# Placing the large loads behind an edge exchange on the sync queue, in a fused coupled-map-lattice, NCA and gate kernel

## The chip, the cores and the metric

The kernel runs on one core of a Trainium2 chip. The metric is the device time of one execution in microseconds. Times inside an execution come from its hardware profile. Engines are named as there: PE is TensorE, DVE is VectorE, ACT is ScalarE, POOL is GpSimd, SP is SyncE, which does nothing here but issue DMAs.

## The reference

Input is x, 32 images of 8 channels and 256 x 256 pixels, float32. Layer 0 normalises x by groups and computes three things of it: a coupled map lattice, an NCA, and a gate that mixes the two. Layer 1 is a quantised 3 x 3 convolution.

```python
x0 = group_norm(x)
grid = drive = x0
for _ in range(15):                                   # the lattice
    mapped = 3.9 * grid * (1.0 - grid)
    local = conv3x3(mapped, K_local, per channel)
    grid = 0.85 * (0.7 * mapped + 0.3 * local) + 0.15 * drive
cml = clip(grid, 0.0001, 0.9999)
nca = sigmoid(conv1x1(relu(conv3x3(x0, Wp, bp)), Wu, bu))
gin = concatenate([x0, cml, nca])                     # 24 channels
g = sigmoid(conv1x1(relu(conv3x3(gin, Wg1, bg1)), Wg2, bg2))
x = x + g * cml + (1.0 - g) * nca
x = x + dequantised(conv3x3(quantised(group_norm(x)), quantised(weight))) + bias
```

## The kernel before

The images are worked on in 8 groups of 4. The first large stage (`one`) runs for each group g three kinds of work beside one another: the lattice of group g, the NCA of the same group, and the gate of group g-1; the normalisation of group g+1 (`prep`) goes in between. Python generators emit the instructions of these, and `together` and `both` weave them by the weights that each `yield` gives. The order on PE is the order of emission (`manual_schedule` for PE); on the other engines and on the sync queue a scheduler places the instructions ahead of the run, in an order near that of emission, and each queue is then worked off in order. The last group's gate runs alone after the last lattice, and a second stage (`two`) does layer 1.

**Lattice.** One unit is one channel of the four images of a group, in two streams s = 0 and s = 1 of two images each; a unit has 15 steps, and in each step `half` runs for s = 0 and then for s = 1. A half is 16 small matmul pairs into PSUM on PE (L502) with three tiny `mark` matmuls (L277), two DVE operations that add the drive (L513), and two that apply the map (L523). The state has two layouts. In a half of the kind a2b, which holds if step + s is even, it goes from `m_a` to `m_b`, and POOL masks the edge columns (L528). In the other kind it goes from `m_b` to `m_a`, and `exchange` copies the edge rows between tiles inside `m_a` by two DMAs on the sync queue (L477, L478). The stream's next half reads `m_a`, so PE waits for these DMAs if they are late. Between a half and the next one of the same stream lies one half of the other stream.

`background(4)` issues up to four queued small DMAs after each half: loads of the next unit's drive (`d_a`, `d_b`) and stores of the last unit's result (L465).

**NCA.** An image has 8 tiles of 32 rows. `rows` loads a tile into one of two buffers `im` by four DMAs of 384 KB (L569), one tile ahead: it is called for tile t+1 after the first matmul group of tile t. `hidden` runs the 3 x 3 convolution on PE (L588), ACT applies the relu into `h` (L596), and `drain` does the 1 x 1 convolution (L604).

**Gate.** Also 8 tiles an image. `inputs` loads `gin` and `gnc` by three DMAs of 384 KB (L665, two buffers), one tile ahead; `blend` loads `mix` by two (L675, one buffer). PE convolves `gin` and `gnc` (L767); `arrange` computes from `mix` on ACT (L688) and POOL (L690, L692) what DVE then combines with the gate (L725, L726). Steps of one tile that are off PE are put into `chores`, of which `together` runs one after each half.

All of these DMAs, and the stores of the normalisation, of the NCA and of the gate, are issued on the sync queue.

Of the kernel before, what the change touches and what calls it, by code (L numbers as in the profile page):

```python
# [31 lines left out]
F32 = mybir.dt.float32  # L32
# [8 lines left out]
P = 128  # L41
C = 8
# [11 lines left out]
ROW = 2 * C * W  # L54
PART = PROWS * C * W
# [5 lines left out]
NBUF = 3 * GB  # L61
# [48 lines left out]
def kernel(  # L110
# [15 lines left out]
    nc = tc.nc  # L126
# [3 lines left out]
    def dram_ap(t, offset, dims):  # L130
        return bass.AP(t.tensor, t.offset + offset, dims)
# [30 lines left out]
    xp_s = [dp.tile([PROWS, 2, C, W], F32, name=f"xp_s{i}") for i in range(NBUF)]  # L162
# [3 lines left out]
    with tc.tile_pool(name="prep", bufs=1) as pp, tc.tile_pool(name="prep2", bufs=2) as pp2:  # L166
# [23 lines left out]
        for t, at, n, w, rows in (  # L190
# [4 lines left out]
            k = 64  # L195
# [59 lines left out]
    with ExitStack() as one:  # L255
# [30 lines left out]
        m_a = [fixed([P, TU, NJ + 2], f"m_a{i}") for i in range(2)]  # L286
# [108 lines left out]
        def lattice(g):  # L395
# [67 lines left out]
            def background(n):  # L463
                for _ in range(min(n, len(later))):
                    nc.sync.dma_start(*later.pop(0))  # L465
                    n -= 1
                    issued[0] += 1
                if g == 0 and units.keys() - {0}:
                    for _ in range(min(n, len(borders))):
                        nc.sync.dma_start(*borders.pop(0))  # L470

            def exchange(t):

                t = t.rearrange("p (k t) j -> p k (t j)", k=2)
                n = (NT - 1) * (NJ + 2)
                above, below = slice(0, n), slice(NJ + 2, NJ + 2 + n)
                nc.sync.dma_start(t[0::16, :, below], t[14::16, :, above])  # L477
                nc.sync.dma_start(t[15::16, :, above], t[1::16, :, below])  # L478

            JOBS = ((0, 5), (5, 10), (10, 14), (14, 18))  # L480
            HALVES = ((slice(0, 10), 5), (slice(10, 18), 4))
# [1 line left out]
            def half(c, step, s, d, m_a, m_b):  # L483

                a2b = (step + s) % 2 == 0
                n = NJ + 1 if a2b else NJ
                k = 0 if a2b else 1
                two = [unit(), unit()]

                def blocks(j, diagonal, first):  # L490
                    t0, t1 = JOBS[j]
                    pt = two[j // 2][:, j % 2, : (t1 - t0) * n].rearrange("p (t j) -> p t j", j=n)
                    own = m_a[:, t0:t1, 1 : 2 + NJ] if a2b else m_b[:, t0:t1, 0:NJ]
                    beside = m_a[:, t0:t1, 0 : 1 + NJ] if a2b else m_b[:, t0:t1, 1 : 1 + NJ]
                    if diagonal:
                        parts = ((LOW, LOW, k, own), (HIGH, HIGH, k, own))
                    elif a2b:
                        parts = ((LOW, HIGH, k, own), (HIGH, LOW, 2, beside))
                    else:
                        parts = ((HIGH, LOW, k, own), (LOW, HIGH, 2, beside))  # L500
                    for src, dst, w, rhs in parts:
                        T.matmul(pt[dst], lw[src, c, w, dst], rhs[src], start=first, stop=not first)  # L502

                for n_, (o, dg, first) in enumerate(((1, 0, True), (3, 2, True), (0, 1, False), (2, 3, False))):
                    blocks(o, False, first)
                    blocks(dg, True, first)
                    if n_ < len(MARKS):
                        mark(n_)

                gts = []  # L510
                for pt, (ts, w) in zip(two, HALVES):
                    gt = gp.tile([P, 10 * (NJ + 1)], F32, name="gt", tag="gt")[:, : 2 * w * n]
                    V.scalar_tensor_tensor(  # L513
                        gt.rearrange("p (u c) -> p u c", u=2), pt[:, :, : w * n], FLOOR,
                        d[:, ts, :].rearrange("p (u t) j -> p u (t j)", u=2), ALU.max, ALU.add,
                    )
                    gts.append(gt.rearrange("p (t j) -> p t j", j=n))
                for gt, (ts, w) in zip(gts, HALVES):
                    if step == STEPS - 1:
                        V.tensor_scalar(d[:, ts, :], gt, 0.0001, 1.0 - 0.0001, ALU.max, ALU.min)  # L520
                        continue
                    to = m_b[:, ts, :] if a2b else m_a[:, ts, 1 : 1 + NJ]
                    V.scalar_tensor_tensor(to, gt, 1.0, gt, ALU.subtract, ALU.mult)  # L523
                if step == STEPS - 1:
                    return a2b
                if a2b:
                    edge = m_b[:, :, 0 : NJ + 1 : NJ]
                    G.tensor_tensor(edge, edge, junk.unsqueeze(1).to_broadcast([P, TU, 2]), ALU.mult)  # L528
                else:
                    exchange(m_a)  # L530
                return a2b

            if g == 0:
# [24 lines left out]
            stored[g] = issued[0] + len(later)  # L558
            if g == NG - 1:
                background(len(later))  # L560

        ORDER = ((0, 4, 1, 5), (2, 6, 3, 7))

        def rows(b, t):

            im = ims[(NT8 * b + t) % 2]
            for k in range(2):
                for q in range(2):
                    nc.sync.dma_start(  # L569
                        im.bitcast(F32)[64 * q : 64 * q + 48, k, :, 1 : 1 + W],  # L570
                        dram_ap(
                            xp_s[b % NBUF], (32 * t + 16 * k + 8 * q) * ROW, [[W, 48], [ROW, 8], [1, W]]
                        ),
                    )
            return im

        loaded = {}

        def nca(b):
# [43 lines left out]

            ahead = loaded.pop(b, None) or rows(b, 0)
            for t in range(NT8):
                im = ahead
                acc = ps_a.tile([P, 512], F32, name="acc", tag="acc")
                for i in range(4):
                    hs = {}
                    for n in (i, i + 4):  # L630
                        hs[n], hs[n + 8] = hidden([im[64 * q : 64 * q + 48, :, n, :] for q in range(2)])
                        if n == 0:
                            if t < NT8 - 1:
                                ahead = rows(b, t + 1)
                            elif all((b + 1, g) in ready for g in range(4)):
                                loaded[b + 1] = rows(b + 1, 0)
                        yield 1.4
                    if i == 2 and done:
                        nc.sync.dma_start(*done)
                        done = None  # L640
                    if pend:
                        done = drain() or done
                    pend = (acc, t, i, hs)
                    yield 0.9
# [14 lines left out]
        def inputs(b, t):  # L659

            src = gs_s[b % NBUF]
            gin = gip.tile([96, 8, W], F32, name="gin", tag="gin")
            gnc = gip.tile([48, 8, W], F32, name="gnc", tag="gnc")
            for j, to in enumerate((gin[:48], gin[48:], gnc)):
                nc.sync.dma_start(  # L665
                    to, dram_ap(src, j * PART + 32 * t * C * W, [[W, 48], [4 * C * W, 8], [1, W]])
                )
            return gin, gnc

        def blend(b, t):  # L670

            src = gs_s[b % NBUF]
            mix = gip.tile([P, 3, 2, W], F32, name="mix", tag="mix", bufs=1)
            for k in range(2):
                nc.sync.dma_start(  # L675
                    mix[:, :, k, :],
                    dram_ap(src, (32 * t + 16 * k + 1) * C * W, [[W, P], [PART, 3], [1, W]]),
                )
            return mix

        flat = lambda t: t.rearrange("p k w -> p (k w)")

        def arrange(sc, mix):

            d = wk.tile([P, 512], F32, name="d", tag="d", bufs=1)
            f = wk.tile([P, 512], F32, name="f", tag="f", bufs=1)
            halves = (slice(0, W), slice(W, 512))
            S.activation(f, flat(mix[:, 0]), AF.Identity, bias=sc[:, 0:1], scale=sc[:, 2:3])  # L688
            for k, cols in enumerate(halves):
                G.tensor_tensor(d[:, cols], mix[:, 1, k], mix[:, 2, k], ALU.subtract)  # L690
            for k, cols in enumerate(halves):
                G.tensor_tensor(f[:, cols], f[:, cols], mix[:, 2, k], ALU.add)  # L692
            return d, f
# [14 lines left out]
        def gate(b):  # L708
# [36 lines left out]
            sc, ahead = staged.pop(b)  # L745
            last = None
            for t in range(NT8 + 1):
                while chores:
                    chores.pop(0)()
                now = {}  # L750
# [2 lines left out]
                    now["gt"] = opened(two[:, 1, :], last["r1"])  # L753
                    now["was"] = last
                if t < NT8:
                    (gin, gnc), mix = ahead
                    if t < NT8 - 1:
                        now["ahead"] = [inputs(b, t + 1)]
                    elif (b + 1) % GB:
# [18 lines left out]
                    was["y"] = mixed(now["gt"], *was["df"])  # L778

                def arrange_(now):  # L780
                    now["df"] = arrange(sc, now["mix"])

                def blend_(now):
                    if now["t"] < NT8 - 1:
# [24 lines left out]
                ahead = now.get("ahead")  # L809
# [89 lines left out]
        for g in range(NG):  # L899
            fill, t = images(nca, g), T_NCA  # L900
            if g:
                fill, t = both(fill, t, after(g - 1, images(gate, g - 1)), T_GATE), t + T_GATE
            if g + 1 < NG:
                fill, t = both(fill, t, prep(g + 1), T_PREP), t + T_PREP
# [176 lines left out]
```

## Time and profile before

| | |
|---|---|
| median of 3 runs | 12252.35 us (12244.07 to 12260.76) |
| profiled execution | 12231.09 us, of it span 12229.3 us |
| PE busy | 10809.9 us, 88% of the span |
| DVE, ACT, POOL busy | 7826.2, 3791.0, 1577.2 us |
| mean granted PE clock | 0.948 |
| DMA queue q1 (the sync queue) | 1651.64 MB, 66.0% of 16 engines' span |

The span is the time from the first to the last instruction of the program; the profiled execution's own time is 1.8 us more. The first group's lattice lasts until about 1585 us, the last one's until about 11280 us. In a line of a group of instructions, the fields are line, engine, operation, out<-in, shapes, count, then busy time in us, mean ns of one, and the idle time of the engine before them with what ended most of it. In a line of a timeline the first two numbers are start and duration in us, and brackets hold the idle time before and its releaser. In a line of the waits: engine and instruction, what it waited for, then total us, times and longest us. In a line of windows: the stretch, its length, then busy us and count for PE, PEld, DVE, ACT and POOL, the granted PE clock, the DMA engines' busy share and GB/s.

### The profile page before, as it was taken

The numbers are of one execution on the slowest core, as the hardware profiler recorded it, in microseconds if no ns is written. First come the engines' busy times: TensorE is split into PE (matmuls) and PEld (weight loads), VectorE is DVE, ScalarE is ACT, GpSimd is POOL, SyncE is SP. The second block draws the span as 40 slices with busy tenths as digits, with TensorE's granted clock in tenths as the row PEclk, the third lists the DMA queues.
The fourth block names the chain that finished last, engine by engine and source line by source line (L and its number), as shares of the span: only waits on it lengthen the run. The fifth ranks groups of instructions, "written<-read, shape, count | busy, mean of one in ns | idle before, by whom it ended". The sixth has DMA issues, their size and how long they took to land. (4 is left out here: it accounts for less than half of the span.)

```text
span 12229.3 us, 289998 instructions
## 1 busy us (share of the span) xinstructions
PE 10809.9 (88%) x124192; PEld 6033.0 (49%) x124192; DVE 7826.2 (64%) x11376; ACT 3791.0 (31%) x4034; POOL 1577.2 (13%) x2242
## 2 busy tenths in 40 slices
PE   4888899999999999999999999999999999999854
PEld 2544555555555555555555555555555555554222
DVE  4655666666666666666666666666666666665377
ACT  2222233332333333333333333333333333332133
POOL 1000011111111111111111111111111111111200
PEclk7999999999999999999999999999999999999776
DMA  6545567766777667766776667777677666665988
GB/s 171 97 98 102 101 136 147 143 140 138 147 142 148 137 137 145 151 141 134 148 151 139 135 140 147 143 145 149 133 146 149 141 133 129 126 123 114 204 249 259
DMA packets 2473159, 1759.74 MB, mean 144 GB/s; under 512 B 1021280, under 2 KB 2442944, under 8 KB 2471744
## 3 DMA queue, kind: packets, MB, share of 16 engines
q1 hardware_dynamic: 2380096, 1651.64, 66.0%
q10 hardware_dynamic: 91776, 89.53, 2.3%
q8 instruction: 979, 16.04, 0.6%
q14 instruction: 308, 2.52, 0.1%
HBM read 1130.62 MB, written 473.89 MB: 131 GB/s over the span
## 5 line engine op out<-in xcount | busy, mean ns | idle before, releaser
L596 ACT ACTIVATE h<-pt,bp_sb 128x1024 f32<-128x1024 f32 x2048 | 2275.6, 1113 | 4947.7 <-PE pt L588 4944.3
L588 PE MATMUL pt<-im,wp_hi 48*128 48x512 f32 x12288 | 2631.8, 424 | 165.4 <-ACT h L596 116.6
L502 PE MATMUL pt<-m_a,lw 64*64 64x325 f32 (+1 forms) x30720 | 2299.3, 433 | 464.9 <-DMA m_a<-m_a 410.1
L513 DVE SCALAR_TENSOR_TENSOR gt<-pt,d_b 128x650 f32<-128x650 f32 (+1 forms) x1920 | 1463.5, 763 | 1945.0 <-PE pt L502 1931.7
L588 PE MATMUL pt<-im,wp_lo 48*128 48x512 f32 x12288 | 2442.5, 393 | 0.2 <-issue 0.2
L513 DVE SCALAR_TENSOR_TENSOR gt<-pt,d_a 128x640 f32<-128x640 f32 (+1 forms) x1920 | 1447.2, 754 | 1531.5 <-PE pt L502 1528.2
L502 PE MATMUL pt<-m_b,lw 64*64 64x320 f32 (+1 forms) x30720 | 2200.5, 417 | 118.1 <-DVE gt L513 82.1
L502 PEld LDWEIGHTS pt<-m_a,lw 64*64 64x64 f32 x30720 | 1316.6, 138 | 1193.2 <-issue 596.9
L588 PEld LDWEIGHTS pt<-im,wp_hi 48*128 48x128 f32 x12288 | 1163.6, 185 | 1275.4 <-issue 719.4
L502 PEld LDWEIGHTS pt<-m_b,lw 64*64 64x64 f32 x30720 | 1237.4, 134 | 858.4 <-issue 463.5
L523 DVE SCALAR_TENSOR_TENSOR m_a<-gt 128x640 f32<-128x640 f32 (+1 forms) x1792 | 1431.7, 799 | 58.6
L523 DVE SCALAR_TENSOR_TENSOR m_b<-gt 128x650 f32<-128x650 f32 (+1 forms) x1792 | 1384.6, 774 | 101.3 <-DVE gt L513 2.8
L528 POOL TENSOR_TENSOR m_b<-m_b,junk 128x36 f32<-128x36 f32 x896 | 243.8, 272 | 7994.9 <-DVE m_b L523 5672.1
L588 PEld LDWEIGHTS pt<-im,wp_lo 48*128 48x128 f32 x12288 | 1168.7, 186 | 201.7 <-issue 0.6
L604 PE MATMUL acc<-h,wu_z 128*32 128x512 f32 x8192 | 1107.7, 612 | 0.0
L767 PE MATMUL pt<-gin,gw 96*32 96x384 f32 (+2 forms) x10240 | 772.0, 450 | 201.3 <-ACT gate L719 178.0
L277 PE MATMUL mark<-qw 64*64 64x1 bf16 x5760 | 947.6, 165 | 0.0
L277 PEld LDWEIGHTS <-qw 64*64 64x64 bf16 x5760 | 632.4, 110 | 205.4 <-issue 9.8
L767 PE MATMUL pt<-gnc,gw 48*32 48x126 f32 (+2 forms) x10240 | 733.1, 429 | 0.0
L767 PEld LDWEIGHTS pt<-gin,gw 96*32 96x32 f32 x10240 | 313.8, 115 | 823.7 <-issue 425.2
L690 POOL TENSOR_TENSOR d<-mix 128x256 f32<-128x256 f32 x512 | 552.1, 1095 | 1240.8 <-DVE gate L725 840.1
L767 PEld LDWEIGHTS pt<-gnc,gw 48*32 48x32 f32 x10240 | 295.0, 108 | 420.8 <-issue 415.3
(110 smaller groups left out, 5939.0 us busy)
## 6 DMA issues: line engine op xcount, KB each, us to landing
im<-xp_s SPq DMA_DIRECT2D x1024, 384.0 KB
gin<-gs_s SPq DMA_DIRECT2D x512, 384.0 KB
mix<-gs_s SPq DMA_DIRECT2D x512, 384.0 KB
gnc<-gs_s SPq DMA_DIRECT2D x256, 384.0 KB
d_a<-gs_s SPq DMA_DIRECT2D x2048, 36.0 KB
yb<-y_s ACTq DMA_DIRECT2D x28, 2432.0 KB
xr<-in_x_dram SPq DMA_DIRECT2D x128, 512.0 KB
xp_s<-hi SPq DMA_DIRECT2D x256, 256.0 KB
```

The lines of the kernel that those rows point to most:

```text
L277: T.matmul(one_[dst], qw[src, 0, dst], qw[src, 0, 0:1], start=True, stop=True)
L502: T.matmul(pt[dst], lw[src, c, w, dst], rhs[src], start=first, stop=not first)
L513: V.scalar_tensor_tensor(gt.rearrange("p (u c) -> p u c", u=2), pt[:, :, : w * n], FLOOR, d[:, ts, :].rearrange("p (u t) j -> p u (t j)", ...
L523: V.scalar_tensor_tensor(to, gt, 1.0, gt, ALU.subtract, ALU.mult)
L528: G.tensor_tensor(edge, edge, junk.unsqueeze(1).to_broadcast([P, TU, 2]), ALU.mult)
L588: T.matmul(ph[:, i, :].rearrange("p (h w) -> p h w", w=W), w[64 * i : 64 * i + 48, dx, :], rhs[:, :, dx : dx + W], start=(dx == 0 and w is ...
L596: S.activation(h.rearrange("p i c -> p (i c)"), ph.rearrange("p i c -> p (i c)"), AF.Relu, bias=bp_sb)
L604: T.matmul(acc[32 * g : 32 * g + 32], wu_z[:, 24 - 8 * i : 56 - 8 * i], hs[4 * g + i], start=(i == 0), stop=(i == 3),)
L690: G.tensor_tensor(d[:, cols], mix[:, 1, k], mix[:, 2, k], ALU.subtract)
L767: T.matmul(three[32 * i : 32 * i + 32, :, to], gw[:rows_, j, dx, :], src[:, i::4, of], start=(j == 0 and n == 0), stop=(j == 1 and n == le ...
```

## The change

`rows`, `inputs` and `blend` no longer issue their loads. Each returns a list of jobs, a job being a size in KB and the arguments of the DMA, and `ask` puts these into a list `asked`. `exchange` returns its second DMA, and `feed` then takes jobs from the front of `asked` as long as a budget of 1200 KB is above zero, and issues them with a scheduling dependency (without a semaphore) on that DMA, so that they stand behind it on the sync queue. Where a tile's computation is emitted, `settle` issues those of its jobs that no exchange has taken yet. After the last lattice `ask` issues at once, as before. Neither the DMAs nor the buffers nor any computation change.

```diff
--- before.py
+++ after.py
@@ -469,13 +469,22 @@
                     for _ in range(min(n, len(borders))):
                         nc.sync.dma_start(*borders.pop(0))
 
+            def feed(behind):
+
+                room = 1200
+                while asked and room > 0:
+                    job = asked.pop(0)
+                    if job[1]:
+                        room -= job[0]
+                        tc.add_manual_dep(begun(job).ins, behind.ins.name, BEHIND, reason="behind the exchange")
+
             def exchange(t):
 
                 t = t.rearrange("p (k t) j -> p k (t j)", k=2)
                 n = (NT - 1) * (NJ + 2)
                 above, below = slice(0, n), slice(NJ + 2, NJ + 2 + n)
                 nc.sync.dma_start(t[0::16, :, below], t[14::16, :, above])
-                nc.sync.dma_start(t[15::16, :, above], t[1::16, :, below])
+                return nc.sync.dma_start(t[15::16, :, above], t[1::16, :, below])
 
             JOBS = ((0, 5), (5, 10), (10, 14), (14, 18))
             HALVES = ((slice(0, 10), 5), (slice(10, 18), 4))
@@ -527,7 +536,7 @@
                     edge = m_b[:, :, 0 : NJ + 1 : NJ]
                     G.tensor_tensor(edge, edge, junk.unsqueeze(1).to_broadcast([P, TU, 2]), ALU.mult)
                 else:
-                    exchange(m_a)
+                    feed(exchange(m_a))
                 return a2b
 
             if g == 0:
@@ -558,21 +567,50 @@
             stored[g] = issued[0] + len(later)
             if g == NG - 1:
                 background(len(later))
+                alone.append(True)
+                settle(asked)
 
         ORDER = ((0, 4, 1, 5), (2, 6, 3, 7))
 
+        asked, alone = [], []
+        BEHIND = mybir.DependencyInfo(mybir.DependencyClass.NoSync, mybir.DependencyReason.DATA)
+
+        def begun(job):
+            args, job[1] = job[1], None
+            return nc.sync.dma_start(*args)
+
+        def settle(jobs):
+            for job in jobs:
+                if job[1]:
+                    begun(job)
+
+        def ask(jobs):
+            if alone:
+                settle(jobs)
+            else:
+                asked.extend(jobs)
+            return jobs
+
         def rows(b, t):
 
             im = ims[(NT8 * b + t) % 2]
-            for k in range(2):
-                for q in range(2):
-                    nc.sync.dma_start(
-                        im.bitcast(F32)[64 * q : 64 * q + 48, k, :, 1 : 1 + W],
-                        dram_ap(
-                            xp_s[b % NBUF], (32 * t + 16 * k + 8 * q) * ROW, [[W, 48], [ROW, 8], [1, W]]
+            return im, ask(
+                [
+                    [
+                        384,
+                        (
+                            im.bitcast(F32)[64 * q : 64 * q + 48, k, :, 1 : 1 + W],
+                            dram_ap(
+                                xp_s[b % NBUF],
+                                (32 * t + 16 * k + 8 * q) * ROW,
+                                [[W, 48], [ROW, 8], [1, W]],
+                            ),
                         ),
-                    )
-            return im
+                    ]
+                    for k in range(2)
+                    for q in range(2)
+                ]
+            )
 
         loaded = {}
 
@@ -623,7 +661,8 @@
 
             ahead = loaded.pop(b, None) or rows(b, 0)
             for t in range(NT8):
-                im = ahead
+                im, jobs = ahead
+                settle(jobs)
                 acc = ps_a.tile([P, 512], F32, name="acc", tag="acc")
                 for i in range(4):
                     hs = {}
@@ -661,26 +700,38 @@
             src = gs_s[b % NBUF]
             gin = gip.tile([96, 8, W], F32, name="gin", tag="gin")
             gnc = gip.tile([48, 8, W], F32, name="gnc", tag="gnc")
-            for j, to in enumerate((gin[:48], gin[48:], gnc)):
-                nc.sync.dma_start(
-                    to, dram_ap(src, j * PART + 32 * t * C * W, [[W, 48], [4 * C * W, 8], [1, W]])
-                )
-            return gin, gnc
+            return gin, gnc, ask(
+                [
+                    [
+                        384,
+                        (to, dram_ap(src, j * PART + 32 * t * C * W, [[W, 48], [4 * C * W, 8], [1, W]])),
+                    ]
+                    for j, to in enumerate((gin[:48], gin[48:], gnc))
+                ]
+            )
 
         def blend(b, t):
 
             src = gs_s[b % NBUF]
             mix = gip.tile([P, 3, 2, W], F32, name="mix", tag="mix", bufs=1)
-            for k in range(2):
-                nc.sync.dma_start(
-                    mix[:, :, k, :],
-                    dram_ap(src, (32 * t + 16 * k + 1) * C * W, [[W, P], [PART, 3], [1, W]]),
-                )
-            return mix
+            return mix, ask(
+                [
+                    [
+                        384,
+                        (
+                            mix[:, :, k, :],
+                            dram_ap(src, (32 * t + 16 * k + 1) * C * W, [[W, P], [PART, 3], [1, W]]),
+                        ),
+                    ]
+                    for k in range(2)
+                ]
+            )
 
         flat = lambda t: t.rearrange("p k w -> p (k w)")
 
-        def arrange(sc, mix):
+        def arrange(sc, mix, jobs):
+
+            settle(jobs)
 
             d = wk.tile([P, 512], F32, name="d", tag="d", bufs=1)
             f = wk.tile([P, 512], F32, name="f", tag="f", bufs=1)
@@ -753,7 +804,8 @@
                     now["gt"] = opened(two[:, 1, :], last["r1"])
                     now["was"] = last
                 if t < NT8:
-                    (gin, gnc), mix = ahead
+                    (gin, gnc, jobs), mix = ahead
+                    settle(jobs)
                     if t < NT8 - 1:
                         now["ahead"] = [inputs(b, t + 1)]
                     elif (b + 1) % GB:
@@ -778,7 +830,7 @@
                     was["y"] = mixed(now["gt"], *was["df"])
 
                 def arrange_(now):
-                    now["df"] = arrange(sc, now["mix"])
+                    now["df"] = arrange(sc, *now["mix"])
 
                 def blend_(now):
                     if now["t"] < NT8 - 1:
```

## The prediction

> **What bounds the kernel now.** I read the page first, then the windows by stage, the waits, and the timeline around the long PE gaps.
>
> ```profile
> PE 10809.9 (88%) x124192; PEld 6033.0 (49%) x124192; DVE 7826.2 (64%) x11376; ACT 3791.0 (31%) x4034; POOL 1577.2 (13%) x2242
> L502 PE MATMUL pt<-m_a,lw 64*64 64x325 f32 (+1 forms) x30720 | 2299.3, 433 | 464.9 <-DMA m_a<-m_a 410.1
> q1 hardware_dynamic: 2380096, 1651.64, 66.0%
> ```
>
> ```profile
> 200.00:1585.00 1385.00, 1169.98 (x13004) 695.88 (x13002) 820.71 (x1197) 391.96 (x381) 79.33 (x148) 0.92 0.51 99
> 1585.00:11280.00 9695.00, 9022.83 (x106937) 5078.63 (x106937) 6328.65 (x9410) 3072.90 (x3205) 1336.05 (x1886) 0.98 0.70 140
> ```
>
> From 1585 to 11280 us PE is busy 93% of the time: in the lattice stage PE sets the pace, and whatever stops it is paid almost in full. The largest stop is the exchange: 410.1 us of PE waiting for m_a<-m_a. That is all that this change can win back directly. All large loads share q1 with the exchange.
>
> The waits of the sync queue's own instructions show the place where SP stands most, at the first DMA of an exchange, for the DVE result. It is idle there, not overloaded:
>
> ```profile
> SPq L477 <- DVE m_a L523: 3298.4, 732, 14.8
> ```
>
> How a load hurts is best seen where the kernel before already does what the change makes a rule: four im loads right behind an exchange. The sync queue's timeline, then PE's, then windows of the clock (the value after POOL):
>
> ```profile
> 5424.63 0.63 SPq L477 DMA_DIRECT2D m_a<-m_a  x1
> 5425.31 0.62 SPq L478 DMA_DIRECT2D m_a<-m_a  x1
> 5426.03 1.93 SPq L569 DMA_DIRECT2D im<-xp_s  x4
> 5428.40 0.62 SPq L477 DMA_DIRECT2D m_a<-m_a  x1
> ```
>
> ```profile
> 5431.88 0.39 PE L588 MATMUL pt<-im,wp_lo 48*128 48x512 f32 x2
> 5438.98 1.79 PE L502 MATMUL pt<-m_a,lw 64*64 64x325 f32 x11 [6.71 <-DMA m_a<-m_a]
> ```
>
> ```profile
> 5424.00:5432.00 8.00, 7.88 (x98) 4.88 (x93) 6.06 (x9) 2.57 (x3) 0.00 (x0) 1.00 0.71 113
> 5432.00:5439.00 7.00, 0.29 (x7) 0.05 (x3) 0.43 (x1) 1.11 (x1) 0.25 (x1) 0.68 1.12 177
> 5439.00:5446.00 7.00, 7.00 (x53) 4.55 (x57) 3.08 (x5) 0.35 (x1) 0.25 (x1) 0.59 0.58 170
> ```
>
> The loads delay not the exchange that they follow but the next one, issued 3.77 us after it: PE stands 6.71 us, and then runs at a clock of 0.59.
>
> **Exchanges come in pairs.** The two lattice streams alternate, so a half with s=1 (even step) and the very next half with s=0 (odd step) both end in an exchange, and the two halves after these have none. By the issue times of the trace the second exchange of a pair follows 4.8 us (median) after the first, and the next pair 17.2 us later. In the trace's DMA packets 2112 bytes is a size that only the exchange has (28,672 packets, 16 for each of 1,792 DMAs), so its landing can be read: 2.3 us after issue if undisturbed, over 6.4 us for a tenth, up to 10.9. PE needs the second exchange 2 us (median) later than the undisturbed landing allows; that much delay is free.
>
> **What moves.** 1024 im, 768 gin/gnc and 512 mix loads, 384 KB each. The budget of 1200 is checked before each load, so four go behind one exchange (1200, 816, 432, 48 are all positive): 1.57 MB, not 1.2. I stepped through the loops with their weights. Loads are asked for during a whole round and the first exchange of a pair comes after the long gap, so it takes most: 1386 of the 2091 placed loads, against 705 behind second ones. Of 448 first exchanges 260 get four loads, 64 three, 77 two, 47 none. That is the wrong one of the pair: 4.8 us of room instead of 17.2.
>
> **What a burst costs.** Four im loads alone take 11.8 us (median of 217 bursts in the packets) from first issue to last landing, near 2.35 us each plus 1 us of start and the issue times: 133 GB/s. Behind a first exchange they are issued from 1.3 us on, so the queue is busy until 1.3+1.0+4x2.35 = 11.7 us; the second exchange could start at 4.8+1.0 = 5.8, so it is 5.9 us late, 3.9 more than is free at the medians. Pairs further apart pay less. Three gin loads: busy until 9.3, 3.5 late, 1.5 not free. Two mix loads (1.7 us each): busy until 5.7, nothing.
>
> [...]
>
> **The sum of the exchange waits.** I went through all 896 exchanges with their issue times of before, the queue taken as first in, first out at the prices above. For the order of before this gives 366 us of PE waiting, where the trace has 410. With the loads moved: first exchanges 143 -> 46 us (the gain that the change is after); second exchanges 223 -> 854, of which 572 behind four loads (260 x 2.2), 197 behind three, 67 behind two, 18 behind none. Net **+534 us**. A second price comes from the trace alone: the 36 second exchanges after 1585 us that had four loads between them and the first cost 2.15 us each, the 61 with three 0.76, the 16 with two 0.13, the 313 with none 0.01. 260x2.15 + 64x0.76 + 77x0.13 = 618, plus 46 for the first ones, minus 410: +254. Its three-load cases sat 9.9 us after the first exchange, not 4.8, so I take the first sum, and this one for the low end.
>
> **The clock.** In the trace all 44 PE gaps of 3 us or more in the lattice are followed by half clock, on average 4.2 us of it after the gap, so 2 us of PE work lost; of 74 gaps of 2 to 2.5 us 53% are. Exchange waits of 3 us or more go from 33 to 140 by the same sum: 107 x 2 = 214, with the shorter ones **+220 us**.
>
> [...]
>
> **Loads that come later.** Median shifts of issue are 10 us for im, 15 for gin, 14 for mix. im still lands over 2.5 us before its tile. In six groups the last gate tile's three gin loads find no exchange left and are issued at their use: 6 x 8.7 = 52 us. mix lands after POOL's present start in 80 tiles (400 us together) and after ACT's in 53 (302 us); nothing of it is on PE unless ACT's h evacuation or POOL's edge operation stands behind it. Bounds 0 and 300; I take 0, since ACT is idle 69% and POOL 87%. Together **+55**. SP gains nothing or loses nothing: it waits for DVE at the exchange anyway, and the loads' buffers are long free when they come. Behind a load stand d_a loads and stores, due a unit later.
>
> **Given back.** PE's other waits in 1585 to 11280 us (ACT h 138, DVE gt 96) shrink when PE stands longer for m_a: a quarter, **-60** (0 to -230).
>
> Sum: 534+220+55-60 = +749. The profiled execution took 12231.1 us (span 12229.3 and 1.8 around it), so 12980; the median of the runs lies 21 us above it, so **13000 us**, 6% slower.
>
> **Rivals.**
> *Faster: the burst is out of the way in time.* It decides if four loads drain in under 6.5 us, or if loads mostly come behind second exchanges. Then all exchange waits fall to what undisturbed landings leave, 49 us: 410-49 = 361 less, and 33 throttles at 2 us and the shorter ones, 90: 11800 us. For it: first exchanges do get free, and 313 undisturbed second ones cost 4 us in all. Against: 11.8 us a burst.
> *No change: the order on SP stays as it was*, because the queue's order is planned and loads drift anyway (at 6017 us gin stands between two exchanges already). Then 12250. Against: the added dependency ties each load behind its exchange.
> *Slower still: late mix holds ACT and POOL,* in order, and h and the edge operation behind it. It decides if more than half of the 302 us on ACT reaches PE, clock losses included: 13300 or more.
>
> **How the numbers follow.** Forecast (second exchanges delayed) 0.78, faster 0.10, no change 0.04, slower still 0.08. Low end: +254 by the trace's own price, half of the clock's 220, nothing else, then 60 back: 12560; I take 12480 for part of the faster case. High end: late mix in full, 13300. A measurement of this kernel tells 0.2% from no change. Faster 0.11, within 0.2% 0.03, slower 0.86.
>
> **What would show it.** Right: PE's wait for m_a near 900 us, nearly all in halves with s=0; a granted clock of 0.95 to 0.96 for 1585 to 11280 us instead of 0.98; PE busy time up by some 200 us with the same instructions; SP's timeline with four loads between the two exchanges of a pair. Wrong: m_a waits under 300 us (the burst drains faster, or sits behind second exchanges); m_a waits as forecast with the span unmoved (other PE waits gave it back); waits of PE for im or gin, or of ACT for mix, above 150 us (lateness, not the queue, is the cost).

## The result and the profile after

The median is 12982.88 us (12978.81 to 13018.55, 4 runs) against 12256.56 us for the kernel before on the same chip: a ratio of 1.0598, 95% interval 1.0575 to 1.0621. The change makes the kernel 6% slower; 13000 us was forecast. The profiled execution has a span of 12981.5 us, 752.2 more than that of before.

Line numbers have moved: L502 is now L511, L477 and L478 are L486 and L487, L569 is L580, L588 is L626. From the page of the changed kernel:

```profile
PE 11069.0 (85%) x124192; PEld 6188.4 (48%) x124192; DVE 7792.4 (60%) x11376; ACT 3786.1 (29%) x4034; POOL 1550.2 (12%) x2242
L511 PE MATMUL pt<-m_a,lw 64*64 64x325 f32 (+1 forms) x30720 | 2528.6, 467 | 1005.8 <-DMA m_a<-m_a 933.3
q1 hardware_dynamic: 2380096, 1651.64, 62.8%
```

The same 124192 matmuls keep PE busy for 259.1 us more, and its idle time (span less busy) goes from 1419.4 to 1912.5 us, 493.1 more. The two make up the 752.2. The wait for the exchange grows by 523.2 us, so more than the whole of the added idle time is there. The bytes on q1 are the same to the last digit.

Its windows by stage, to be read against the two of before (the last lattice now ends near 12030 us; the clock is the value after POOL):

```profile
200.00:1585.00 1385.00, 1198.14 (x13370) 714.26 (x13362) 838.36 (x1220) 402.91 (x392) 86.51 (x158) 0.93 0.52 102
1585.00:12030.00 10445.00, 9252.61 (x106532) 5214.09 (x106529) 6273.16 (x9379) 3053.48 (x3191) 1300.99 (x1876) 0.95 0.66 130
```

The granted clock falls from 0.98 to 0.95 in the long stage and not in the first, where of the moved loads there is almost only im. The wait for the exchange does the same: in the first stage it goes from 165 to 154 us, behind it from 245 to 780. The sync queue's wait at the exchange shrinks (3298.4 us before), probably because it now has loads to issue between the two exchanges of a pair:

```profile
SPq L486 <- DVE m_a L532: 2759.2, 687, 13.4
```

One pair, in the timelines of the sync queue and of PE, and then the windows around it:

```profile
9086.25 0.65 SPq L486 DMA_DIRECT2D m_a<-m_a  x1
9086.95 0.62 SPq L487 DMA_DIRECT2D m_a<-m_a  x1
9087.67 1.92 SPq L580 DMA_DIRECT2D im<-xp_s  x4
9089.70 0.61 SPq L486 DMA_DIRECT2D m_a<-m_a  x1
9090.35 0.60 SPq L487 DMA_DIRECT2D m_a<-m_a  x1
```

```profile
9095.54 0.39 PE L626 MATMUL pt<-im,wp_lo 48*128 48x512 f32 x2
9102.06 1.79 PE L511 MATMUL pt<-m_a,lw 64*64 64x325 f32 x11 [6.13 <-DMA m_a<-m_a]
```

```profile
9093.00:9100.00 7.00, 2.93 (x24) 2.06 (x24) 2.52 (x4) 2.23 (x2) 0.25 (x1) 0.95 1.13 139
9100.00:9107.00 7.00, 4.94 (x43) 2.66 (x43) 1.37 (x2) 0.00 (x0) 0.00 (x0) 0.56 0.38 107
```

The second exchange follows the first by 3.45 us; the four loads between them are on the DMA engines (busy share 1.13, 139 GB/s in the first window), and the second exchange lands at 9101.2 us, 11.5 us after its issue. PE stands for 6.13 us and then works at a clock of 0.56. What was one of 49 pairs with four loads in it is now one of 261.

PE's waits for the exchange divide like this (us of waiting; number of exchanges in brackets). The order of the halves on PE tells which exchange a wait is for:

| second exchange, by loads issued since the first | before | after |
|---|---|---|
| none | 3.9 (313) | 6.9 (46) |
| two | 2.1 (16) | 2.2 (77) |
| three | 46.4 (61) | 110.6 (64) |
| four | 174.4 (49) | 733.6 (261) |
| one, five or eight | 26.0 (9) | 0 (0) |
| all second exchanges | 252.9 (448) | 853.2 (448) |
| all first exchanges | 157.2 (448) | 80.1 (448) |

### The profile page after: what moved, and what is told of

Its sections match the earlier page's. It is cut to its first block, busy times and chain, and to the rows that moved or that the text cites. A ratio compares the mean times of both kernels' runs of the same rounds, so it can differ in the third digit from the quotient of the medians.

```text
span 12981.5 us, 289751 instructions
## 1 busy us (share of the span) xinstructions
PE 11069.0 (85%) x124192; PEld 6188.4 (48%) x124192; DVE 7792.4 (60%) x11376; ACT 3786.1 (29%) x4034; POOL 1550.2 (12%) x2242
## 5 line engine op out<-in xcount | busy, mean ns | idle before, releaser
L511 PE MATMUL pt<-m_a,lw 64*64 64x325 f32 (+1 forms) x30720 | 2528.6, 467 | 1005.8 <-DMA m_a<-m_a 933.3
L626 PE MATMUL pt<-im,wp_hi 48*128 48x512 f32 x12288 | 2642.6, 426 | 158.8 <-ACT h L634 91.6
L626 PE MATMUL pt<-im,wp_lo 48*128 48x512 f32 x12288 | 2447.6, 394 | 0.0
L511 PEld LDWEIGHTS pt<-m_a,lw 64*64 64x64 f32 x30720 | 1472.9, 149 | 1794.0 <-issue 1217.3
L511 PE MATMUL pt<-m_b,lw 64*64 64x320 f32 (+1 forms) x30720 | 2179.3, 415 | 64.9 <-DVE gt L522 41.8
L626 PEld LDWEIGHTS pt<-im,wp_hi 48*128 48x128 f32 x12288 | 1170.0, 186 | 1287.4 <-issue 753.3
L511 PEld LDWEIGHTS pt<-m_b,lw 64*64 64x64 f32 x30720 | 1230.0, 133 | 797.3 <-issue 415.0
L626 PEld LDWEIGHTS pt<-im,wp_lo 48*128 48x128 f32 x12288 | 1174.9, 187 | 201.4
L819 PE MATMUL pt<-gin,gw 96*32 96x384 f32 (+2 forms) x10240 | 779.4, 453 | 204.8 <-ACT gate L770 173.8
L819 PE MATMUL pt<-gnc,gw 48*32 48x384 f32 (+2 forms) x10240 | 744.8, 435 | 3.2 <-DMA gnc<-gs_s 3.2
L819 PEld LDWEIGHTS pt<-gin,gw 96*32 96x32 f32 x10240 | 317.7, 116 | 829.4 <-issue 431.4
L741 POOL TENSOR_TENSOR d<-mix 128x256 f32<-128x256 f32 x512 | 523.1, 1035 | 1430.3 <-DVE gate L776 832.5
L819 PEld LDWEIGHTS pt<-gnc,gw 48*32 48x32 f32 x10240 | 297.6, 109 | 432.8 <-issue 424.8
```

Source lines behind the costliest of these rows:

```text
L626: T.matmul(ph[:, i, :].rearrange("p (h w) -> p h w", w=W), w[64 * i : 64 * i + 48, dx, :], rhs[:, :, dx : dx + W], start=(dx == 0 and w is ...
L819: T.matmul(three[32 * i : 32 * i + 32, :, to], gw[:rows_, j, dx, :], src[:, i::4, of], start=(j == 0 and n == 0), stop=(j == 1 and n == le ...
```

## The experiments

Two theories stood against each other, with a third beside them. **Q**: a burst of loads is still being moved when the next exchange is issued, and delays it. **L**: the loads come later than before, and their users (PE for im and gin, ACT and POOL for mix) wait. **S**: the same DMAs in another planned order cost time on SP or shift the other engines' order. The kernel before gave 12257.58 us beside the first four runs, 12261.92 beside the next three and 12269.43 beside the last two. Line numbers move by a few from run to run: the lattice's matmuls stand at L509 to L511, those of the NCA near L626, those of the gate near L819.

**Behind the second exchange alone.**

```diff
-            def feed(behind):
-
-                room = 1200
+            def feed(behind, room):
+
...
-                    feed(exchange(m_a))
+                    feed(exchange(m_a), 2400 if s == 0 else 0)
```

> All moved loads stand behind the second exchange of a pair alone, budget 2400 KB (up to seven loads), none behind the first. Theory Q (the burst of loads in the queue delays the next exchange): the second exchange follows the first with nothing between, so PE's wait for it falls from 853 us to under 30; bursts of seven last about 17 us, as long as the median gap to the next pair, so first exchanges take over part of it, 250 to 450 us. Time 12450 to 12750 us, faster than the changed kernel by 250 us or more. Rival L (loads that come later hold up PE, ACT and POOL): loads come later still than in the changed kernel, so the time is at or above 12980 us.

12680.98 us, ratio 1.0351 (1.0328 to 1.0374): 302 us below the changed kernel with later loads, which L excludes. PE's waits:

```profile
PE pt L510 <- DMA m_a<-m_a: 596.7, 141, 13.2
PE pt L818 <- DMA gin<-gs_s: 110.3, 30, 5.6
```

Of the 596.7 us, 22.1 are at second exchanges, as Q has it. The 574.6 at first exchanges are above the 250 to 450 expected: 440.6 of them come at the 112 that follow seven loads. At 57 of these over 500 packets are still to be moved when the next pair comes. Lateness is real but small: gin's wait on PE is 110.3 us, where the kernel before has 23.3.

**Behind the first exchange alone.**

```diff
-                    feed(exchange(m_a))
+                    feed(exchange(m_a), 2400 if s == 1 else 0)
```

> The mirror of the run before: budget 2400 KB behind the first exchange of a pair alone, none behind the second. The same loads, about as late. Theory Q: up to seven loads (17 us) stand before the second exchange 4.8 us later; PE waits for it 1700 to 2300 us in all, the granted clock in the lattice falls below 0.90, and the time is 13900 to 14500 us. Rival L: as lateness is like that of the run before, so is the time, within 200 us of it.

14299.06 us, ratio 1.1664 (1.1638 to 1.169). The mirror differs from the run before in nothing but which of two exchanges the loads follow, and is 1618 us slower.

```profile
PE pt L510 <- DMA m_a<-m_a: 1903.6, 377, 14.2
POOL d L740 <- DMA mix<-gs_s: 1063.8, 252, 16.4
1585.00:13316.00 11731.00, 9563.78 (x107435) 5376.95 (x107435) 6323.68 (x9454) 3076.02 (x3215) 1273.09 (x1891) 0.90 0.59 116
```

The three lines are two of the waits and a window. Q's numbers hold: 1903.6 us, of it 1855.4 at second exchanges, and a clock of 0.90, where a little below 0.90 was expected. POOL's wait for mix grew too, but hardly reached PE: PE's idle time in the whole span is 1516 us above that of the kernel before, and its wait for the exchange alone 1493.

**Half the bytes of im.**

```diff
-                            im.bitcast(F32)[64 * q : 64 * q + 48, k, :, 1 : 1 + W],
+                            im.bitcast(F32)[64 * q : 64 * q + 48, k, 0:4, 1 : 1 + W],
...
-                                [[W, 48], [ROW, 8], [1, W]],
+                                [[W, 48], [ROW, 4], [1, W]],
```

> The changed kernel with half of the bytes in each im load (rows 4 to 7 of each tile part are left out, the im buffers zeroed once instead): order, number of DMAs and budget as they are. Theory Q: a burst of four im loads is out of the queue after about 1.3+1.0+4x1.2 = 7 us instead of 11.7, so the second exchange is about 1 us late, which is free; bursts of gin, gnc and mix stay. PE's wait for m_a falls from 933 to 450 to 650 us, the time to 12450 to 12700 us. Rival L: im was never late, so nothing changes beyond 100 us. Rival S (the cost is SP's issue and waits, or another order on the other engines): nothing changes either, as the instructions are the same.

12298.69 us, ratio 1.0029 (1.0014 to 1.0044), with the same DMAs and matmuls in the same placement; the kernel leaves out half of im's rows, so half of the bytes and half of the 1024-byte packets. S and L expected no effect; 684 us of the 726 are gone. Q missed its ranges on the low side, for the time (12450 to 12700) and for the wait (450 to 650):

```profile
PE pt L510 <- DMA m_a<-m_a: 408.2, 190, 7.2
```

Second exchanges with four loads before them (261 again) cost 231.3 us instead of 733.6. Fewer bytes help in other places too (PE's wait for all other exchanges is 176.9 us, in the changed kernel 199.7; POOL's for mix 376.0 and 446.0), and the kernel before was not run with half of them, so this run overstates im's share; but the same issues in the same order cost next to nothing once less has to be moved. Bytes and packets are halved together here, so which of the two counts is not shown.

**The exchange on another queue** (the kernel before, with `nc.scalar.dma_start` for both DMAs of `exchange`).

```diff
-                nc.sync.dma_start(t[0::16, :, below], t[14::16, :, above])
-                nc.sync.dma_start(t[15::16, :, above], t[1::16, :, below])
+                nc.scalar.dma_start(t[0::16, :, below], t[14::16, :, above])
+                nc.scalar.dma_start(t[15::16, :, above], t[1::16, :, below])
```

> The kernel before, with the two DMAs of an exchange on ACT's queue instead of the sync queue; the large loads stay where they were. Theory Q, in its form that standing behind the loads in the same queue is the cost: exchanges no longer wait for the loads, PE's wait for m_a falls from 410 to under 150 us although the same bytes move, a gain of up to 300 us less what ACT pays for 1792 issues of 0.6 us and for standing at them. Rival B (the 16 DMA engines' bandwidth is the limit, whatever the queue): the wait for m_a stays above 300 us. Time 11900 to 12500 us by Q, above 12250 by B.

13178.14 us, ratio 1.0749 (1.0718 to 1.078). Q fell here in the form that the text gave it, and B held:

```profile
PE pt L502 <- DMA m_a<-m_a: 413.3, 160, 8.3
ACT h L596 <- DMA m_a<-m_a: 614.1, 141, 10.1
PE pt L588 <- ACT h L596: 303.1, 360, 4.4
```

The wait for the exchange is 413.3 us, as with one queue (410.1). In the packets, all 28,672 of the exchange are on q10 now. Where 200 to 400 packets of 1024 bytes start within 2.2 us of an exchange's issue, it lands after 5.56 us on the mean (258 cases); on the shared queue it was 5.58 us (248 cases). The own queue did not get past the loads. The packets show it directly. Where over 500 of the 1024-byte packets issued ahead of an exchange had not started at its issue, and none were issued in the 2.5 us after it, 99% of these started before the exchange's last packet on either arrangement (183 cases, 195 on the shared queue). And loads issued after it delayed the exchange on its own queue as well: with nothing left from before but three or more loads' worth (1152 KB) issued in the 2.5 us after it, the exchange lands after 4.19 us (48 cases), on the shared queue after 2.31 (46).

The loss of 920 us is another matter. PE is busy 421 us longer at a lower clock (0.922), and of its added 546 us of idle time 352 are waits for ACT's `h` (303.1 us in L588, as above, and 202.5 in L502, where the kernel before has 116.6 and 37.2). That `h` now stands behind the exchange's issue in ACT's order is likely from the 614.1 us that ACT waits for m_a before `h`; it was not tried by itself.

**One load behind the first, up to five behind the second.**

```diff
-                    feed(exchange(m_a))
+                    feed(exchange(m_a), 1900 if s == 0 else 300)
```

> The changed kernel with a budget that fits the room: one load behind the first exchange of a pair (drained 1.3+1.0+2.35 = 4.7 us after it, before the second exchange could start at 5.8) and up to five behind the second (about 13.5 us, inside the median 17 to 19 us to the next pair). Theory Q: PE's wait for m_a falls to 100 to 250 us, below the 410 of the kernel before; loads are later than in the changed kernel, so gin's waits on PE are 50 to 150 us, as in the run with loads behind second exchanges alone. Time 12100 to 12400 us, at or near the kernel before, 600 us or more below the changed kernel. Rival L (lateness is the cost): no better than the run with loads behind second exchanges alone, 12680 us.

12337.82 us, ratio 1.0065 (1.0039 to 1.0092): 645 us below the changed kernel and inside the range, so the size of the burst against the room decides. The wait of 268.4 us for the exchange is above the 100 to 250 expected:

```profile
PE 10927.5 (89%) x124192; PEld 6089.5 (49%) x124192; DVE 7846.3 (64%) x11376; ACT 3785.2 (31%) x4034; POOL 1553.2 (13%) x2242
PE pt L510 <- DMA m_a<-m_a: 268.4, 111, 8.4
PE pt L818 <- DMA gnc<-gs_s: 42.2, 17, 3.5
PE pt L625 <- DMA im<-xp_s: 41.8, 16, 15.8
PE pt L818 <- DMA gin<-gs_s: 34.1, 19, 3.7
```

It waits 142 us less for the exchange than the kernel before and is still 0.65% slower. Here L has its share: gin, gnc and im hold PE for 118 us (41 before), its idle time is 1408.5 us in all, only 11 less than before, and PE is busy 117.6 us longer, at a lower clock (0.940, 0.948 before). The lower clock is most of the loss, and its cause is open: PE works 235 us more at half clock in the lattice, nearly all of it around gaps of 1.5 to 3 us, of which there are 137 where the kernel before has 120. Placement behind exchanges buys short exchange waits with waits for the loads.

**im alone, and the gate's loads alone** (the other part calls `ask` with `move=False`, which issues at once).

```diff
-        def ask(jobs):
-            if alone:
+        def ask(jobs, move=True):
+            if alone or not move:
```

> One part of the change alone: im's loads are listed and placed behind an exchange, gin, gnc and mix are issued where they were before. Theory Q: an im tile is always asked for as four loads, and most of the 256 bursts land behind a first exchange at about 2.8 us of PE waiting each; the wait for m_a is 700 to 950 us, nearly that of the whole change, and the time 12650 to 12950 us. Rival L: im is never late for its tile, so im alone costs nothing: 12250 to 12350 us.

> The other part alone: gin, gnc and mix are listed and placed, im's loads are issued where they were before. Theory Q: bursts of three gin and gnc loads cost 1.7 us each behind a first exchange and pairs of mix nothing, while im's bursts go on to hit exchanges as in the kernel before; the wait for m_a is 400 to 650 us, the time 12300 to 12600 us. Rival L: the gate's loads are the ones that come late (mix on ACT and POOL, the last tile's gin), so this part holds nearly all of the loss, 12800 us or more.

im alone: 12759.64 us, ratio 1.0405 (1.038 to 1.043). The gate's loads alone: 12664.45 us, ratio 1.0319 (1.0284 to 1.0354). The first line is of im alone, the second one, from another profile, of the gate's loads alone:

```profile
PE pt L511 <- DMA m_a<-m_a: 873.5, 224, 9.5
```

```profile
PE pt L511 <- DMA m_a<-m_a: 631.2, 203, 12.4
```

Both waits are inside what Q expected; the gate's time is 64 us above its range. L's figures (12350 us at most, and 12800 or more) fit neither. im alone costs 458 us at 145 second exchanges with four loads before them, 3.2 us each, and 245 us at 32 with seven. The losses of the parts (498 and 402 us) add up to more than the whole (726). The 32 show a reason: in the changed kernel no second exchange has more than four loads before it, but here the loads that are not listed still fall between the two exchanges, together with those that are.

**Holding back only what would fall into a pair.** Loads are issued at once as in the kernel before, except those asked for between the two exchanges of a pair, which are put behind the second, without a budget; in the second kernel, from one half earlier. The lines below are of the first of the two.

```diff
+                    behind = exchange(m_a)
+                    if s == 1:
+                        held.append(True)
+                    else:
+                        held.clear()
+                        feed(behind)
...
-            if alone:
+            if not held:
                 settle(jobs)
```

> Only the loads that are asked for between the two exchanges of a pair (by the loops' weights 59 of 256 im tiles, 69 gin, 42 mix) are held back until the second exchange and placed behind it; all others are issued at once, as in the kernel before. Theory Q: the 260 us that PE waits for second exchanges in the kernel before fall to under 60, first exchanges stay near 150, and the held loads are at most some 5 us late, so nothing else waits longer; the clock gains 50 to 100 us. PE's wait for m_a 150 to 260 us, time 11900 to 12100 us: faster than both kernels. Rival S (the planned order shifts other loads into the gap, or the queues of ACT, POOL and DVE lose what PE gains): 12200 us or more.

> As the run before, but loads are held from one half earlier on, from the half ahead of the first exchange of a pair (112 im, 36 gin and 84 mix tiles more). Theory Q: first exchanges are freed too (150 us to under 80), but more loads gather behind a second exchange, up to seven and more, which reach the next pair when it comes early: PE's wait for m_a 120 to 300 us. Loads are held up to 11 us, so gin and mix begin to be late. Time 11900 to 12250 us, not clearly better than the run before. Rival S: 12200 us or more.

The first: 12201.05 us, ratio 0.9943 (0.9922 to 0.9965), faster than both kernels, but only 68 us below the one before; 11900 to 12100 us were expected. The second: 12320.18 us, ratio 1.0049 (1.0033 to 1.0065), above its 11900 to 12250. The m_a waits of the one and of the other, both above what was expected (150 to 260 and 120 to 300):

```profile
PE pt L509 <- DMA m_a<-m_a: 352.0, 152, 9.5
```

```profile
PE pt L509 <- DMA m_a<-m_a: 500.5, 162, 9.9
```

Second exchanges are freed as forecast: 12.2 and 20.4 us instead of 252.9. First exchanges take most or all of it back, 339.8 and 480.1 us instead of 157.2; in the second kernel 349.3 of them come after seven loads since the last exchange. In the first kernel they come after four (93.3 us, all but 0.2 in the first group's lattice) and after five (134.2 us). Of the 95 exchanges after five loads, 54 have over 500 packets still to be moved when they are issued, where the kernel before has 20 of 62; the last of the five loads is issued 1.8 us ahead of the exchange (median), 14.8 before. What moved these issues was not tried, and both times are at or above the 12200 us that S set as its mark, so a part for the planned order (S) is not excluded here. With 2304 loads of 384 KB to place, no rule tried here keeps both exchanges free.

## Why the prediction was right

**The place.** "The loads delay not the exchange that they follow but the next one": shown by the mirror, 12681 against 14299 us. The counts of the loops' order held to within one: 261, 64, 77 and 46 second exchanges behind four, three, two and no loads, 260, 64, 77 and 47 forecast.

**The exchange waits.** +534 us were forecast (366 to 900 in the arithmetic), +523.2 measured (410.1 to 933.3). The terms inside were off and balanced: four loads cost 2.8 us each, not 2.2; three 1.7, not 3.1; two nothing, where 67 us stood; first exchanges kept 80 us, not 46. That second exchanges come to 853 us where 854 stood is luck. The "second price", from the 36 natural cases of before, gave +254: its 2.15 us for four loads was low (2.56 after the first group's lattice in the changed kernel), it left out the 13 cases of that lattice, which cost 7.5 us each, and its 0.76 us for three came from pairs far apart, as the text feared. The counts of 61, 16 and 313 beside the 36 are of the whole trace and not of the part after 1585 us.

**The clock.** +220 us were forecast. The clock records show half clock while PE worked for 437 us of the lattice before and 965 after; half of the difference, 264 us, is close to the growth of PE's busy time there (257.9). Gaps of 3 us and more went as forecast: 97 more (44 to 141, 107 forecast), and if each stretch of half clock is put down to the longest gap just before or in it, they cost 208 us (214 forecast). The part that was too small is that of the shorter gaps, 56 us where 6 stood, mostly gaps of 1.5 to 3 us.

**The rate of the loads.** The trace's 133 GB/s for these loads gave the loss that came. The run with half the bytes shows that the size of the loss hangs on what a burst has to move (0.3% instead of 6%); a gain from this placement was seen in no run.

**Loads that come later.** 55 us were forecast, 52 of them for gin at 8.7 us a time in six places. That term was too large: PE's wait for gin grew from 23.3 to 31.0 us, the longest is 3.5 us, gnc adds 3.2, and the wait for im did not grow. mix was later as forecast, on POOL 147.1 to 446.0 us and on ACT 103.7 to 311.6, and the 0 taken for it held: PE's waits for ACT's h fell. The text had named a wait of ACT for mix above 150 us as a sign that lateness is the cost. It came, and the conclusion would have been false; the sign should have been PE's wait for what ACT makes of mix. The first lines are of the kernel before, the others of the changed one:

```profile
POOL d L690 <- DMA mix<-gs_s: 147.1, 36, 15.6
ACT f L688 <- DMA mix<-gs_s: 103.7, 20, 12.3
PE pt L767 <- DMA gin<-gs_s: 23.3, 7, 8.3
PE pt L588 <- ACT h L596: 116.6, 84, 2.1
```

```profile
POOL d L741 <- DMA mix<-gs_s: 446.0, 135, 12.7
ACT f L739 <- DMA mix<-gs_s: 311.6, 62, 10.3
PE pt L819 <- DMA gin<-gs_s: 31.0, 16, 3.5
PE pt L626 <- ACT h L634: 91.6, 75, 2.1
```

**Given back.** 60 us forecast. All added idle time in the lattice is 492.1 us where m_a alone added 523.2 and gin and gnc 11, so 42 came back. Measured less forecast, the four terms are off by -11, +38, -44 and +18 us; that their sum of 749 meets the 752.2 of the profiled executions is in part luck.

**What the mechanism was called.** The text placed the cost in the sync queue that loads and exchange share. The run with the exchange on ACT's queue shows that the shared queue is not needed for it: the landings are as late on a queue of their own (5.56 us, 5.58 on the shared one). The arithmetic survives, as it only used that what is issued first is moved first, which the packets show on both arrangements (99% of the 1024-byte packets that were waiting, 183 and 195 cases); the reason stated for it does not.

## What to carry to other kernels

In this kernel a transfer that others wait for was delayed by the loads that were still to be moved when it was issued, on both of the queues that were tried. So large loads are placed by the time until the next critical transfer, at the rate that the trace shows for these very loads (133 GB/s here), and not right behind the last one: a burst of 11.8 us put into a gap of 4.8 us cost 2.8 us of waiting, on the mean, at each of 261 exchanges. Such waits cost twice on PE here, once as idle time (523 us more) and once as half clock after it (264 us more).

## What the runs showed of the hardware

An exchange on a hardware queue of its own landed no sooner than in the loads' queue (5.56 against 5.58 us with loads moving, 2.3 us undisturbed), and loads issued after it delayed it too (4.19 us against 2.31 on the shared queue). Where over 500 of the loads' 1024-byte packets were waiting at its issue, 99% of them started before its last packet, on its own queue (183 cases) as on the shared one (195). What keeps this order stays open.
